# Two attention layers on one core: where the matrix engine passes from one layer to the next

## The chip, the cores and the metric

The kernel runs on one core of one Trainium2 chip. Time is device time in microseconds (us), the median of several executions. Beside it stands one profiled execution, from whose trace all durations below are taken. A core has a matrix engine (PE, with its weight loads shown apart as PEld), a vector engine (DVE), an activation engine (ACT), a general engine (POOL) and a queue that issues most DMAs (SP).

## What is computed

The input x is (4, 128, 64, 64): four batches of 128 channels and 4096 positions. All numbers are 32-bit floats. Layer 0 is an attention of 64 channels with a residual; layer 1 turns to tokens, takes a layer norm, a causal attention of 128 channels with a residual, another norm, and a recurrence over the tokens with batch statistics.

```python
q, k, v = wq @ x, wk @ x, wv @ x                 # 64 x 4096 per batch
att = softmax(einsum('bmi,bmj->bij', k, q), axis=2)
x = x + wo @ einsum('bij,bmj->bmi', att, v)      # layer 0
t = tokens(x)                                    # 4096 x 128 per batch
h = layernorm(t)
t = t + causal_softmax((h Wq)(h Wk)^T / sqrt(128)) @ (h Wv)   # layer 1
w = batchnorm(layernorm(t) @ W^T)
y_t = sigmoid(w_t + y_{t-1} @ V^T)               # over 4096 steps
x = channels(t + y)
```

## The kernel before, in words

Only `fast_path` matters here; `general_path` is a branch that runs when a check of the numbers fails. The end of `fast_path` (the recurrence, from line 1113 on) is untouched by the change.

**Blocks and items.** The work of both attentions is one list. For each batch b, `block` (lines 887 to 902) lists four blocks of layer 0, each of 32 items, and then eight blocks of layer 1, the block g having 2(g+1) items: a block is 512 rows of one output (two such halves at once in layer 0), an item is one tile of 128 keys in layer 0 and two tiles in layer 1. The last two items of each layer 1 block lie on the causal diagonal and are shorter (512+384 and 256+128 columns).

**What an item does.** `scores` (904) multiplies keys by rows on PE into a buffer of the pool `ps_s` (two buffers), and ACT takes the exponential of it into `p` (four buffers); on the diagonal POOL then zeroes a triangle. `sums` (943) adds p into `dsum` on DVE, for the denominators. `values` (963) multiplies values by p on PE into `acc`, of which there is one buffer; at the end of a block ACT copies `acc` out. In layer 0 each item's matmuls go to the four 64x64 quarters of the array, four at a time; in layer 1 they use the whole 128x128 array.

**The loop** (1073 to 1106). In slot s the program issues the scores of item s, the values of item s-2 (`SKEW` is 2), the sums of item s, and then at most one waiting step for each layer, or one of the tasks in the list `side`. So where one layer follows the other, scores of the new layer stand between the last values of the old one. `begin` (1061) issues the scores; after the first block of layer 0 it is called one slot early (lines 1075 to 1078).

**The end of a block.** `finish0` (734) folds the denominators, and later `projected0` (646, 64x64 matmuls) applies the output projection to a pair of row groups and `joining` adds the residual, takes the norm (`moments`, `normed`) and writes its transpose `xhT` by DMA. When that projection runs is set by the table `visits` (1012): the projection of layer 0's pair 0, 1, 2 is issued at the end of layer 0's block 1, 2, 3, and that of pair 3 at the end of layer 1's block 2. `finish1` (777) is a chain of steps a few slots apart: denominators and `projected1` (639, 128x128), norm, transposition, and `third` (842), which multiplies by the FFN's W.

**Rows.** `rows()` (1034) prepares the rows of one block, one block in advance, at each block's end. For layer 0 it costs nothing; for layer 1 it is `rows1` (594), one 512-column product `r_ps` on the whole array, copied out by ACT. So the product for layer 1's block 0 is issued at the end of layer 0's block 2, and that for its block 1 at the end of layer 0's block 3.

**The next batch.** `keys(b, m)` (1020) makes the keys, queries (`cols0`, 128x128) and values (`vals0`, 128x64) of a quarter of a batch. For batch 0 they are done before and in layer 0's first slots, for the others in layer 1's blocks from g=3 on, through `side`.

**What is shared.** Every small product above takes its output from `misc` (489), a pool of two PSUM buffers: `kr_ps`, `v_ps`, `r_ps`, `o_ps`, `den_ps`, `wx_ps` and some others. `projected0` takes both at once and holds them until `joined` (662, DVE) has read them.

**What sets the order.** The program's order is a priority: a planner at build time puts the instructions of each engine in a fixed order by its own estimate of when each can run, and keeps the order only where the program pins it. At run time each engine takes its instructions in that order and waits.

Of the kernel before, what the change touches and what calls it, by code (L numbers as in the profile page):

```python
# [359 lines left out]
def fast_path(  # L360
# [27 lines left out]
    NB = N // BLK  # L388
# [92 lines left out]
    with tc.tile_pool(name="batch", bufs=1) as batch, tc.tile_pool(name="rows", bufs=2) as rowp, tc.tile_pool(  # L481
# [35 lines left out]
        bs = [Batch() for _ in range(B)]  # L517
        for bt in bs:
            bt.next = []
            bt.leave = {}  # L520


        def cols0(b, m):
# [109 lines left out]
        def denominators(layer, b, g, own):  # L633
            rec = recs[:, layer, b, ts(g, TPB)]

            tc.keep_in_program_order(nc.vector.tensor_reduce(rec, own.rearrange("p q j -> p j q"), AX.X, ALU.add))
            nc.vector.reciprocal(rec, rec)

        def projected1(agg):

            op = misc("o_ps")
            for j in range(TPB):
                nc.tensor.matmul(op[:, ts(j, P)], lhsT=agg[:, ts(j, P)], rhs=wv1, start=True, stop=True)  # L643
            return op

        def projected0(agg):

            ops = [misc("o_ps") for _ in range(2)]
            for j in range(TPB):
                for r in range(2):  # L650
                    part = slice(r * M, r * M + M)
                    for c in range(2):
                        nc.tensor.matmul(  # L653
                            ops[r][c * M : c * M + M, ts(j, P)],
                            lhsT=agg[part, ds(j * P + c * M, M)],
                            rhs=wo2[part],
                            start=True,
                            stop=True,
                        )
            return ops  # L660

        def joined(layer, b, g, op):

            rec = recs[:, layer, b, ts(g, TPB)]
            for j in range(TPB):
                t = xs[:, b, ds(g * BLK + j * P, P)]
                nc.vector.scalar_tensor_tensor(  # L667
                    t, in0=op[:, ts(j, P)], scalar=rec[:, j : j + 1], in1=t, op0=ALU.mult, op1=ALU.add
                )
# [64 lines left out]
        def finish0(b, pair):  # L734

            agg, den = bs[b].agg, bs[b].den
            own = {}

            def first(k):
                own[k] = folded(den[:, k], False)  # L740

            def joining(g, op):
                mem = []

                def norm():
                    if g == 0:
                        bs[b].xh = batch.tile([P, NT, P], F32, tag="xh", name="xh")
                    normed(b, g, bs[b].xh[:, ts(g, TPB)], *mem.pop())

                def by_channels():  # L750
                    sq = squares(bs[b].xh[:, ts(g, TPB)])
                    by_r = dram2.tile([S, Q, TPB, Q, S], F32, tag="by_r", name="by_r")
                    for q in range(Q):
                        nc.sync.dma_start(
                            out=by_r[:, :, :, q].rearrange("r c j t -> r (c j) t"),
                            in_=sq[ts(q, S)].rearrange("r c j t -> r (c j) t"),
                        )
                    for c in range(Q):
                        nc.sync.dma_start(
                            out=bs[b].xhT[ts(c, S), ts(g, BLK)], in_=by_r[:, c].rearrange("r j q t -> r (j q t)")  # L760
                        )

                yield 1, lambda: joined(0, b, g, op)
                yield 1 + 4 * (g % 2), lambda: mem.append(moments(b, g))
                yield 1, norm
                yield 2, by_channels

            def leave():
                ops = projected0(agg)
                return [joining(2 * pair + k, op) for k, op in enumerate(ops)]  # L770

            bs[b].leave[pair] = leave
            yield 1, lambda: first(0)
            yield 2, lambda: first(1)
            yield 6, lambda: [denominators(0, b, 2 * pair + k, own[k]) for k in range(2)]

        def finish1(b, g):
            agg, den = bs[b].agg, bs[b].den
            mem = {}
            final = b == B - 1 and g == NB - 1  # L780
# [9 lines left out]
            def first():  # L790
                if final:

                    nc.scalar.activation(spare, agg[:, 0:1], AF.Sigmoid)
                denominators(1, b, g, mem["own"])
                joined(1, b, g, projected1(agg))
                if final:
                    warm(9, agg[:, : BLK // 2])
                if b >= BY_C:
                    nc.sync.dma_start(
                        out=x2t[b - BY_C, ts(g, BLK)].rearrange("(j p) c -> p j c", p=P),  # L800
                        in_=xs[:, b, ts(g, BLK)].rearrange("p (j c) -> p j c", c=P),
                    )
                mem["xh"] = wk.tile([P, TPB, P], F32, tag="xh2", name="xh2")
                mem["of"] = moments(b, g)
                if final:
                    in_range(True)
# [59 lines left out]
            def sums():  # L866
                mem["own"] = folded(den, by_pe)

            if by_pe:
                yield 1, lambda: (sums(), first(), final and norm())  # L870
            else:
                yield 1, sums
                yield 3, first
# [2 lines left out]
            yield 2, second  # L876
            if b < BY_C:
                yield 1, kept
            yield 1 if final else 6 if g < 2 or g == NB - 1 else 4, third


        class Item:
# [2 lines left out]
        items, blocks = [], []  # L885
# [10 lines left out]
        for b in range(B):  # L896
            for g in range(NB // 2):
                block(0, b, g, range(NT))
            for g in range(NB):
                full = [((t, 0, BLK), (t + 1, 0, BLK)) for t in range(0, TPB * g, 2)]  # L900
                d = [(TPB * g + r, r * P, BLK - r * P) for r in range(TPB)]
                block(1, b, g, full + [(d[0], d[1]), (d[2], d[3])])
# [106 lines left out]
        waiting = [[], []]  # L1009


        visits = [{1: 0, 2: 1, 3: 2}, {2: 3}]
        assert NB == 8

        def push(slot, layer, chain):
# [4 lines left out]
        def keys(b, m):  # L1020
# [4 lines left out]
                lambda: b or vals0_by_tokens(b, m, mem[0]),  # L1025
            ]

        parts = [keys(0, m) for m in range(NB // 2)]
        for task in parts[0][:2] + parts[1][:1] + parts[0][2:]:
            task()  # L1030
        SKEW = 2
        side = parts[1][1:] + parts[2] + parts[3] + [form]

        def rows():

# [20 lines left out]
        started = []  # L1056
        rows()
        rows()
        done = -1

        def begin(s):
            nonlocal done
            if done < s < len(items):
                done = s
                it = items[s]
                if it.first:
                    bs[it.b].rows = bs[it.b].next.pop(0)
                    if it.layer and it.g == 3 and it.b + 1 < B:
                        for m in range(NB // 2):
                            side.extend(keys(it.b + 1, m))  # L1070
                scores(it)

        for s in range(len(items) + SKEW + 16):
            begin(s)
            if SKEW < s < len(items) - 1 and items[s - SKEW].first and items[s + 1].layer == 0:
                ended = items[s - SKEW - 1]
                if ended.layer == 0 and ended.g not in visits[0]:
                    begin(s + 1)
            if 0 <= s - SKEW < len(items):
                it = items[s - SKEW]  # L1080
                values(it)
                if it.last:
                    if it.g in visits[it.layer]:
                        for chain in bs[it.b].leave[visits[it.layer][it.g]]():
                            push(s, 0, chain)
                    rows()
                    tokens()
                    push(s, it.layer, (finish1 if it.layer else finish0)(it.b, it.g))
            if s < len(items):
                sums(items[s])  # L1090
            busy = False
            for layer in range(2):
                due = [w for w in waiting[layer] if w[0] <= s]
                if due:
                    busy = True
                    w = min(due, key=lambda w: w[0])
                    waiting[layer].remove(w)
                    w[1]()
                    push(s, layer, w[2])
            if side and not busy:  # L1100
                side.pop(0)()
                if not side and items[s].b == 0 and items[s].layer == 0:
                    tokens()
                    load_rest()
                    form_half()
        assert not any(waiting) and not side


# [213 lines left out]
```

## Time and profile before

| | |
|---|---|
| median of 3 runs | 2058.08 us (2057.14 to 2059.81) |
| the profiled execution | 2057.13 us |
| its span, first to last instruction | 2055.4 us |
| PE busy | 2026.6 us (99%), weight loads 912.4 us |
| DVE busy | 1454.5 us (71%) |
| ACT busy | 976.1 us (47%) |
| POOL busy | 139.8 us (7%) |
| one layer 0 item on PE, from start to start | 1.72 us |
| one full layer 1 item on PE | 3.43 us |

The ends of PE's matmuls in the records are modelled and overlap the next matmul, so "busy" includes waiting time. Starts are observed; the distances between starts are what the text uses.

### The profile page before, as it was taken

What the parts mean: (1) busy time and instruction counts of PE and PEld (TensorE: products, weight loads), DVE (VectorE), ACT (ScalarE), POOL (GpSimd) and SP (SyncE); (2) the same over time, 40 slices, a digit from 0 to 9 for tenths busy, and PEclk for the clock granted to TensorE, in tenths of its full rate; (3) what the DMA queues carried; (4) which work ended last, traced back from release to release, by engine and by line L of the source; (5) the groups of instructions that cost most, each with busy time, mean ns of one, the idle gap of its engine ahead of it and who ended that gap; (6) DMA issues with size and microseconds to landing.
All of it is one profiled execution on the core that took longest, in us unless ns stands there. A gap on an engine that the chain in (4) does not pass through costs nothing.

```text
span 2055.4 us, 31316 instructions
## 1 busy us (share of the span) xinstructions
PE 2026.6 (99%) x11902; PEld 912.4 (44%) x11902; DVE 1454.5 (71%) x2814; ACT 976.1 (47%) x1055; POOL 139.8 (7%) x237
## 2 busy tenths in 40 slices
PE   9999999999999999999999999999999999999998
PEld 3463344444333345444433334444433334444456
DVE  4788887554778877655577888655577887865568
ACT  4665633333666643333466663332356665333346
POOL 1000011000000001000000001000000000100004
PEclk9999999999999999999999999999999999999999
DMA  3101122330011103331110111232000100220046
GB/s 103 53 2 23 22 45 54 69 72 16 17 43 23 19 5 62 72 67 37 20 44 12 22 22 40 54 83 62 16 17 2 18 12 17 55 50 21 16 103 242
DMA packets 238447, 89.06 MB, mean 43 GB/s; under 512 B 174816, under 2 KB 219360, under 8 KB 237776
## 3 DMA queue, kind: packets, MB, share of 16 engines
q1 hardware_dynamic: 237280, 86.42, 17.9%
q8 instruction: 95, 1.56, 0.3%
q14 instruction: 64, 0.52, 0.1%
q0 software_dynamic: 288, 0.39, 0.1%
q10 hardware_dynamic: 720, 0.16, 0.0%
HBM read 45.84 MB, written 36.89 MB: 40 GB/s over the span
## 4 chain that ended last, share of the span: by engine, by line
PE 92%; DVE 4%; ACT 2%; issue 1%; POOL 0%; DVEq 0%; POOLq 0%; ACTq 0%
PE s_ps L926 22%; PE acc L982 22%; PE s_ps L913 20%; PE acc L973 20%; PE o_ps L643 1%; PE r_ps L596 1%; DVE dsum L953 1%; PE kr_ps L534 1%; PE wx_ps L854 1%; DVE z L1188 1%; PE v_ps L546 1%; ACT y L1192 1%; PE o_ps L653 0%; DVE xr L1224 0%; ACT p L920 0%
## 5 line engine op out<-in xcount | busy, mean ns | idle before, releaser
L953 DVE TENSOR_TENSOR dsum<-dsum,p 128x1024 f32<-128x1024 f32 x692 | 845.6, 1222 | 462.2 <-ACT p L929 289.5
L920 ACT ACTIVATE p<-s_ps,nshift 128x1024 f32<-128x1024 f32 x512 | 570.0, 1115 | 314.4 <-PE s_ps L913 288.7
L973 PE MATMUL acc<-p,v 64*64 64x512 f32 x4096 | 643.4, 591 | 0.0
L913 PE MATMUL s_ps<-kr,swap 64*64 64x512 f32 x2048 | 585.8, 591 | 0.3
L913 PE MATMUL s_ps<-kr 64*64 64x512 f32 x2048 | 580.2, 591 | 0.0
L929 ACT ACTIVATE p<-s_ps 128x1024 f32<-128x1024 f32 (+2 forms) x288 | 274.2, 952 | 592.8 <-PE s_ps L926 568.1
L982 PE MATMUL acc<-p,xh 128*128 128x512 f32 (+3 forms) x1152 | 501.1, 558 | 1.4 <-ACT half L996 1.4
L926 PE MATMUL s_ps<-rows,xhT 128*128 128x512 f32 (+3 forms) x1152 | 501.8, 559 | 0.0
L982 PEld LDWEIGHTS acc<-p,xh 128*128 128x128 f32 x1152 | 215.9, 190 | 245.5 <-issue 232.7
L926 PEld LDWEIGHTS s_ps<-rows,xhT 128*128 128x128 f32 x1152 | 214.4, 190 | 247.7 <-issue 208.1
L973 PEld LDWEIGHTS acc<-p,v 64*64 64x64 f32 x4096 | 205.1, 133 | 260.5 <-issue 239.9
L913 PEld LDWEIGHTS s_ps<-kr,swap 64*64 64x64 f32 x2048 | 165.3, 133 | 137.9 <-issue 119.2
L913 PEld LDWEIGHTS s_ps<-kr 64*64 64x64 f32 x2048 | 163.3, 133 | 130.7 <-issue 120.3
L681 POOL TENSOR_TENSOR ln_rstd<-ln_var,mhalf 128x4 f32<-128x4 f32 x64 | 68.2, 1066 | 907.8 <-DVE ln_var L679 907.8
L961 DVE TENSOR_TENSOR dsum<-dsum,p 128x256 f32<-128x256 f32 (+1 forms) x120 | 55.6, 495 | 51.6 <-POOL p L933 51.6
L933 POOL TENSOR_SCALAR_AFFINE_SELECT p<-p 128x128 f32<-128x128 f32 x128 | 36.3, 307 | 602.7 <-ACT p L929 589.3
L667 DVE SCALAR_TENSOR_TENSOR xs<-o_ps,recs,xs 128x128 f32<-128x128 f32 x256 | 70.6, 343 | 3.4 <-PE o_ps L643 0.3
L697 DVE TENSOR_SCALAR xh<-xs,ln_mv,ln_rstd 128x128 f32<-128x128 f32 x252 | 70.0, 341 | 1.8
L676 DVE BATCH_NORM_STATS2 ln_st<-xs 128x6 f32<-128x128 f32 x256 | 64.4, 270 | 0.0
L951 DVE COPY dsum<-p 128x1024 f32<-128x1024 f32 x44 | 30.2, 686 | 28.9 <-ACT p L929 25.6
L859 ACT COPY xs<-wx_ps 128x512 f32<-128x512 f32 x31 | 18.1, 585 | 65.2 <-DVE stats L855 62.0
L596 PE MATMUL r_ps<-xhT,g 128*128 128x512 f32 x64 | 33.6, 607 | 14.2 <-issue 10.4
(149 smaller groups left out, 916.5 us busy)
## 6 DMA issues: line engine op xcount, KB each, us to landing
xs<-in_xT SPq DMA_DIRECT2D x32, 256.0 KB, 3.3
by_r<-sqT SPq DMA_DIRECT2D x128, 64.0 KB, 2.2
xhT<-by_r SPq DMA_DIRECT2D x128, 64.0 KB, 2.0
by_c<-sqT SPq DMA_DIRECT2D x124, 64.0 KB, 1.8
xhT<-by_c SPq DMA_DIRECT2D x31, 256.0 KB, 2.8
xs<-in_x SPq DMA_DIRECT2D x12, 512.0 KB, 6.1
swap<-kr SPq DMA_DIRECT2D x32, 128.0 KB, 2.3
x2c<-sqT SPq DMA_DIRECT2D x64, 64.0 KB, 2.2
```

Source lines behind the costliest of these rows:

```text
L667: nc.vector.scalar_tensor_tensor(t, in0=op[:, ts(j, P)], scalar=rec[:, j : j + 1], in1=t, op0=ALU.mult, op1=ALU.add)
L676: nc.vector.bn_stats(st[:, j], xs[:, b, ds(g * BLK + j * P, P)])
L681: nc.gpsimd.tensor_tensor(y, var, mhalf, ALU.pow)
L697: nc.vector.tensor_scalar(dst[:, j], xs[:, b, ds(g * BLK + j * P, P)], mv[:, j, 0:1], y[:, j : j + 1], ALU.subtract, ALU.mult)
L913: nc.tensor.matmul(ps[c * M : c * M + M, ts(r, BLK)], lhsT=keys[:, ts(c, M)], rhs=rows[r], start=True, stop=True,)
L920: nc.scalar.activation(it.p, ps, AF.Exp, bias=nshift)
L926: nc.tensor.matmul(ps[:, off : off + n], lhsT=lhsT, rhs=rhs, start=True, stop=True)
L929: nc.scalar.activation(it.p[:, :off], ps[:, :off], AF.Exp, scale=float(P) ** -0.5)
L953: nc.vector.tensor_tensor(flat, flat, it.p, ALU.add)
L961: nc.vector.tensor_tensor(den[:, h, q0:], den[:, h, q0:], it.p[:, o : o + n], ALU.add)
L973: nc.tensor.matmul(bt.acc[c * M : c * M + M, r], lhsT=bt.v[part, m * TPB + j, h], rhs=it.p[part, ts(c, BLK)], start=it.first, stop=it.last,)
L982: nc.tensor.matmul(bt.acc[:, 0, q0:], lhsT=bt.xh[:, t], rhs=it.p[:, o : o + n], start=it.first and h == 0, stop=it.last and h == 1,)
```

## The change

- The loop holds back the scores of the first two items of a layer (`turns`) until the values of the old layer's last item, and what else is to be done at that point, have been issued. Sums follow the scores by their own counter.
- The projections of layer 0's pairs 0 to 2 become a step of their own block's chain, 12 slots after the block's end (`yield 3, leave`), in place of the table `visits`. Pair 3 is still projected after layer 1's third block.
- The rows of layer 1's first two blocks are both made at the turn, none at the end of layer 0's block 2.
- Layer 1 takes block 1 before block 0.
- Of the next batch's keys, the last quarter is made at the turn to layer 0; there too goes the projection of layer 1's last block. The last block's product with W (`third`) waits in a list `late` until the next turn to layer 1.
- Scores are begun one slot early at every border between two layer 0 blocks.
- At the start the quarter tasks are run together with pauses, and `form_half` runs 12 slots later.

```diff
@@ finish0
             def leave():
-                ops = projected0(agg)
-                return [joining(2 * pair + k, op) for k, op in enumerate(ops)]
-
-            bs[b].leave[pair] = leave
+                for k, op in enumerate(projected0(agg)):
+                    push(now, 0, joining(2 * pair + k, op))
+
             yield 1, lambda: first(0)
             yield 2, lambda: first(1)
             yield 6, lambda: [denominators(0, b, 2 * pair + k, own[k]) for k in range(2)]
-
-        def finish1(b, g):
+            if pair < NB // 2 - 1:
+                yield 3, leave
+            else:
+                bs[b].leave = leave
+
+        def finish1(b, g, turn):
...
-                joined(1, b, g, projected1(agg))
+                joined(1, b, g, mem["op"] if turn else projected1(agg))
...
+            if turn:
+                mem["op"] = projected1(agg)
             if by_pe:
...
-            yield 1 if final else 6 if g < 2 or g == NB - 1 else 4, third
+            if turn:
+                late.append(third)
+            else:
+                yield 1 if final else 6 if g < 2 else 4, third
...
-            for g in range(NB):
+            for g in (1, 0, *range(2, NB)):
...
-        visits = [{1: 0, 2: 1, 3: 2}, {2: 3}]
...
+        late = []
+        SKEW = 2
         parts = [keys(0, m) for m in range(NB // 2)]
-        for task in parts[0][:2] + parts[1][:1] + parts[0][2:]:
+        for task in parts[0][:2] + parts[1][:1] + parts[0][2:] + parts[1][1:2]:
             task()
-        SKEW = 2
-        side = parts[1][1:] + parts[2] + parts[3] + [form]
+
+        def together(*tasks):
+            return lambda: [task() for task in tasks]
+
+        idle = lambda: None
+        side = [idle, together(parts[1][2], *parts[2][:2]), idle, idle, together(parts[2][2], *parts[3][:2]), idle, idle]
+        side.append(together(parts[3][2], form))
...
-                        for m in range(NB // 2):
+                        for m in range(NB // 2 - 1):
                             side.extend(keys(it.b + 1, m))
                 scores(it)
 
+        def turns(s):
+            return SKEW <= s < len(items) and items[s].layer != items[s - SKEW].layer
+
         for s in range(len(items) + SKEW + 16):
-            begin(s)
-            if SKEW < s < len(items) - 1 and items[s - SKEW].first and items[s + 1].layer == 0:
-                ended = items[s - SKEW - 1]
-                if ended.layer == 0 and ended.g not in visits[0]:
-                    begin(s + 1)
+            now = s
+            if not turns(s):
+                begin(s)
+                if SKEW < s < len(items) - 1 and items[s - SKEW].first and not turns(s + 1):
+                    if items[s].layer == 0 and items[s - SKEW - 1].layer == 0:
+                        begin(s + 1)
             if 0 <= s - SKEW < len(items):
                 it = items[s - SKEW]
                 values(it)
                 if it.last:
-                    if it.g in visits[it.layer]:
-                        for chain in bs[it.b].leave[visits[it.layer][it.g]]():
-                            push(s, 0, chain)
-                    rows()
+                    turn = turns(s)
+                    if it.layer == 0:
+                        push(s, 0, finish0(it.b, it.g))
+                        if turn:
+                            rows()
+                        if not blocks[0][0] or turn:
+                            rows()
+                        while turn and late:
+                            late.pop(0)()
+                    else:
+                        if it.g == 2:
+                            waiting[0].append((s + 1, bs[it.b].leave, iter(())))
+                        if turn:
+                            held = keys(it.b + 1, NB // 2 - 1)
+                            held[0]()
+                        push(s, 1, finish1(it.b, it.g, turn))
+                        if turn:
+                            held[1]()
+                        rows()
                     tokens()
-                    push(s, it.layer, (finish1 if it.layer else finish0)(it.b, it.g))
-            if s < len(items):
-                sums(items[s])
+                    if turn:
+                        begin(s - 1)
+                        begin(s)
+            while summed < min(done, s):
+                summed += 1
+                sums(items[summed])
...
-                    form_half()
+                    waiting[0].append((s + 12, form_half, iter(())))
```

More of the change, by code (lines that the diff above doesn't have):

```diff
@@ L519, in fast_path @@
             bt.next = []
-            bt.leave = {}
         def cols0(b, m):
@@ L1058, in fast_path @@
         rows()
-        done = -1
+        done = summed = -1
         def begin(s):
```

## Prediction

> **What bounds the kernel now.** I read the page's engine shares and chain first, then PE's own waits, then the timeline at every place where PE falls behind its steady pace.
>
> ```profile
> PE 2026.6 (99%) x11902; PEld 912.4 (44%) x11902; DVE 1454.5 (71%) x2814; ACT 976.1 (47%) x1055; POOL 139.8 (7%) x237
> PE 92%; DVE 4%; ACT 2%; issue 1%; POOL 0%; DVEq 0%; POOLq 0%; ACTq 0%
> ```
>
> PE is both the busy engine and the chain. But matmul ends are modelled, so I measure start to start and set it against the work. A 512-column matmul takes 0.427 us (four of them are a steady 1.71 us group in layer 1), four 64x64 quarters sharing one such time; 128-column ones a quarter of it. From 8 to 1975 us the distances between PE's starts add up to about 47 us more than that, the steady pace's own few ns per matmul taken off. The change can win only from those 47 us. Where they lie:
>
> ```profile
> PE r_ps L596 <- issue: 10.4, 4, 2.6
> PE r_ps L596 <- PE acc L982: 3.9, 4, 1.0
> ```
>
> PE's two largest waits: the rows product of layer 1, twice per batch, 14.3 us in all. The timeline at the end of layer 0's third block, batch 1:
>
> ```profile
> 686.68 1.05 PE L653 MATMUL o_ps<-wo,xhT 64*64 64x128 f32 x32
> 687.55 0.60 PE L913 MATMUL s_ps<-kr,swap 64*64 64x512 f32 x2
> ...
> 689.96 2.15 DVE L667 SCALAR_TENSOR_TENSOR xs<-o_ps,recs,xs 128x128 f32<-128x128 f32 x8
> ...
> 691.18 1.10 PE L596 MATMUL r_ps<-xhT,g 128*128 128x512 f32 x2 [2.60 <-issue]
> 692.20 0.64 PE L913 MATMUL s_ps<-kr 64*64 64x512 f32 x1
> ```
>
> The projection (L653) takes both `misc` buffers; r_ps needs one, and the first is free only when four of DVE's eight L667 steps are through (689.96 + 4 x 0.27 = 691.04). PE stands in its fixed order behind r_ps, with a quarter of a score still to do. The turn to layer 1, same batch:
>
> ```profile
> 743.85 1.77 PE L926 MATMUL s_ps<-rows,xhT 128*128 128x512 f32 x4
> 745.55 1.09 PE L973 MATMUL acc<-p,v 64*64 64x512 f32 x8
> 746.57 0.92 PE L926 MATMUL s_ps<-rows,xhT 128*128 128x256 f32 x4
> 747.41 1.09 PE L973 MATMUL acc<-p,v 64*64 64x512 f32 x8
> 748.32 1.05 PE L653 MATMUL o_ps<-wo,xhT 64*64 64x128 f32 x32
> 749.73 2.17 PE L982 MATMUL acc<-p,xh 128*128 128x512 f32 x6 [0.35 <-ACT half L996]
> 751.65 2.15 DVE L667 SCALAR_TENSOR_TENSOR xs<-o_ps,recs,xs 128x128 f32<-128x128 f32 x8
> 752.87 1.10 PE L596 MATMUL r_ps<-xhT,g 128*128 128x512 f32 x2 [0.97 <-PE acc L982]
> 754.89 3.60 PE L926 MATMUL s_ps<-rows,xhT 128*128 128x512 f32 x8
> ```
>
> Five changes of array shape, a wait for `acc`, and the same wait for a `misc` buffer again. The turn to layer 0:
>
> ```profile
> 513.29 0.14 PEld L913 LDWEIGHTS s_ps<-kr,swap 64*64 64x64 f32 x2 [0.76 <-issue]
> 513.29 0.65 PE L913 MATMUL s_ps<-kr,swap 64*64 64x512 f32 x2
> 514.31 1.77 PE L982 MATMUL acc<-p,xh 128*128 128x512 f32 x4
> 516.01 0.65 PE L913 MATMUL s_ps<-kr,swap 64*64 64x512 f32 x2
> ```
>
> Eight quarter matmuls are 0.85 us of work and take 1.02; four full ones of 512+384 columns are 1.49 and take 1.70.
>
> **What the Trainium skill says.** "TensorEngine Tiling (Array Packing)", Key Properties: changing the tiling mode, not just the tile, drains the engine. The trace agrees and prices it: 0.11 to 0.21 us per change, 0.16 on average. "TensorE: Matmul & The Clock Gate", Architectural detail: PE can pull weight loads ahead of running matmuls. In steady stretches the trace shows them 0.43 us ahead; at the change above load and matmul both start at 513.29, so the price is lost prefetch as well as drain. "Trainium Kernel Development and Optimization", Best Practices: steady bubbles can mean that PSUM ran out; the r_ps wait is that. "Perfetto Trace Analysis" says that PE ends are estimated, hence starts here.
>
> **Part by part.**
>
> *Third block and turn to layer 1* (rows moved, pairs' projections moved, scores held back). From the projection at the third block's end to the first full layer 1 scores after r_ps, PE takes 68.21 us in batches 1 to 3 (686.68 to 754.89) and 69.90 in batch 0, for 61.44 of work; steady loss over some 68 groups is 0.4. Avoidable: 6.4, 6.4, 6.4, 8.1, sum 27.2 us. Of a 6.4, 3.2 is the third block (687.55 to 692.20 is 4.65 us for 1.49 of work), the rest the turn. Batch 0's extra 1.7 follows its r_ps, when quarters run out of step.
> What stays: at the turn PE does the last two values, two r_ps, `late` (0.86 us; none in batch 0), then scores. The last values need no wait: their exponential ends about 1.4 us after the scores (0.2 + 1.11), PE has 1.7 us of other values. One change of shape, 0.3 with the lost prefetch. ACT copies `acc` (1.00), then the first rows (0.59): ready about 2.0 us after the last values, PE gets there after 1.7 to 2.6: 0 to 0.3. New: with only two items of block 0 after block 1, r_ps of block 2 is needed at once; its copy waits behind `agg` (0.58) and itself takes 0.8, PE has 0.86 of r_ps and perhaps 1.5 of values: 0 to 0.8. I take 0.9 in all. PE executes in order, so each of these holds up all that follows it on PE, and through the scores ACT's exponentials. The projections themselves stay 0.87 us each, now amid 64x64 work without a change. Gain 27.2 - 4 x 0.9 = 23.6.
>
> *Turn to layer 0, three times.* Losses from 511.5 to 545: alternating 1.07, the projection at 525.14 0.51, W's product at 543.55 0.37; 1.95, of which 0.2 stays (the 128-column loads). After: 128x128, then v_ps in 128x64, then 64x64, two changes (0.35); the projection waits for a `misc` buffer that DVE empties (0.69 + 0.2, against 0.86 of PE work; 0.1); and the pipe refills: two scores are 1.72 us, the first exponential is ready at 0.86 + 0.2 + 1.11 + 0.1 = 2.3, so 0.5. Sum 1.0. In layer 1 one of four v_ps insertions goes (0.3). Gain 3 x (1.75 - 1.0 + 0.15) = 2.7; the 0.15 halves that 0.3, as the quarter's swap and value DMAs (10 more on SP at the turn) might delay token loads. The quarter is needed 24 items later, 41 us, so that they land late matters only past that.
>
> *Start.* Some 8 fewer changes x 0.16 = 1.3, and `form_half` no longer right behind its loads (36 to 41 us loses 0.9). Against it, three bundled tasks chain through two `misc` buffers, 0.2 to 0.9 each. Between -1.5 and +2; I take a gain of 0.7.
>
> *Block borders in layer 0.* Early scores replace the projection as the work that covers the copy of `acc` (1.00 us against 1.72). Block 0's border does so today: 575.56 to 578.99 is exactly four steady groups. 0. If ACT were late there, about 0.5 each, 8 borders.
>
> *DVE.* A pair's chain (joining, moments, norm, transpose; about 13 us with the folds, from the L667, L676, L677, L697, L711, L607, L609 rows) no longer starts with the folds of the next block. Spare DVE time in layer 0 is 1.72 - 1.22 = 0.5 us per slot, and four p buffers hide about 5 us of lag; today it shows as 0.4 us once in three of the batches. Taken as 0, between -2 and +1.2.
>
> Sum: 23.6 + 2.7 + 0.7 = 27.0 us. Against the profiled execution: span 2055.4 to 2028.4, 2057.1 to 2030.1. The median is 0.95 above the profiled run, so 2031.
>
> **Rivals.**
> 1. *Gain half eaten by refills.* At each of seven turns nothing fills PE while the exponential (and POOL's triangles) and ACT's rows copy come. Worst case at a turn to layer 1: 1.4 before the last values, 1.9 for the copies, 0.8 for block 2's rows, 4.1 against 0.9 taken; to layer 0: 1.3 + 1.8 for two evacuations + 1.3, 4.4 against 1.0. Half of that excess is 4 x 1.6 + 3 x 1.7 = 11.5: 2042. For: the planner misjudged r_ps today. Against: the drain's own arithmetic above.
> 2. *The changes of shape alone go, the r_ps waits return elsewhere.* 27.0 - 14.3: 2045.
> 3. *Slower.* The two `misc` buffers collide in layer 1's start: pair 3's projection, W's products of blocks 0 and 1, and the next rows fall within four slots after block 2, while DVE is near full (24.5 busy of 26 us from 764 to 790 today). Each wait costs 3 us like the r_ps one; more than nine, some two or three per batch, cancel the gain; at four per batch, 16 x 3 = 48, 2079. Against: today the same steps meet there (790 to 800) at under 0.2 us each, and 10 us of DVE work, pair 2's chain, leaves that stretch.
> 4. *Nothing*: within 0.2% if the waits only change their names, 2058.
>
> **Numbers.** Likeliest 0.68 (2031, its own range 2024 to 2039), rivals 1 and 2 0.19 together, no change 0.04, slower 0.09. About 0.2% (4 us) is what a measurement of this kernel can tell. Faster 0.87, same 0.04, slower 0.09. The range 2024 to 2047 takes the likeliest and rivals 1 and 2.
>
> **What would show it.** r_ps waits of PE from 14.3 to under 3 us; no 128x128 matmul inside layer 0's 32-item blocks after batch 0's start; 68.21 us becoming about 62.7; one wait of about half a microsecond early in each turn to layer 0. Wrong if new PE waits on `misc` users (o_ps, wx_ps, den_ps) appear in layer 1's first 40 us, or if DVE's lag holds up exponentials after the moved projections.

## The result and the profile after

The changed kernel takes 2028.26 us (median of 4 runs, 2028.15 to 2028.38); the kernel before, on the same chip, takes 2058.03 (4 runs, 2057.14 to 2059.81). The ratio is 0.9854, with a 95% interval of 0.9837 to 0.9871. The forecast was 2031.0, within 2024 to 2047. The profiled execution took 2028.15 us with a span of 2026.4, against 2055.4 before: 29.0 us less.

The page of the kernel after, its engine shares and its chain:

```profile
PE 2011.7 (99%) x11902; PEld 878.3 (43%) x11902; DVE 1459.6 (72%) x2814; ACT 975.9 (48%) x1055; POOL 139.8 (7%) x237
PE 96%; DVE 2%; ACT 2%; DMA 0%; issue 0%; POOL 0%; ACTq 0%; POOLq 0%
```

The same 11902 matmul records; the chain still runs along PE, and DVE's and ACT's shares of it fell from 6% to 4%. One fp32 matmul stands as two records in the trace: layer 0's 512 items make four score matmuls each, and L920 has 4096 records. The prediction's "eight quarter matmuls" are eight such records, four matmuls. PE's waits after (what waits, for what, us in total, times, longest):

```profile
PE warm_ps L495 <- POOL ident masks.py:199: 2.6, 1, 2.6
PE s_ps L920 <- ACT p L927: 1.3, 3, 0.4
```

The two `r_ps` rows, 14.3 us before, are gone. No wait of the attention's blocks is left but the second row: three of 0.4, one per turn to layer 0. The first lies at the program's start, and the rows below these, 1.1 us and less each, at its start and in its last part.

The timeline at the end of layer 0's third block, batch 1 (start, duration, engine, line, operation), where PE stood for 2.60 us before:

```profile
679.61 0.60 PE L920 MATMUL s_ps<-kr,swap 64*64 64x512 f32 x2
...
680.04 1.90 PE L980 MATMUL acc<-p,v 64*64 64x512 f32 x16
681.75 0.60 PE L920 MATMUL s_ps<-kr 64*64 64x512 f32 x2
```

Scores go straight into sixteen value records and back: 1.71 us from 680.04 to 681.75 for 1.71 of work. The turn to layer 1, batch 0:

```profile
245.98 2.75 PE L980 MATMUL acc<-p,v 64*64 64x512 f32 x24
...
248.67 1.98 PE L595 MATMUL r_ps<-xhT,g 128*128 128x512 f32 x4
248.81 1.01 ACT L1003 COPY half<-acc 128x1024 f32<-128x1024 f32 x1 [1.46 <-PE acc L980]
...
249.83 0.59 ACT L597 COPY rows<-r_ps 128x512 f32<-128x512 f32 x1
...
250.49 5.18 PE L933 MATMUL s_ps<-rows,xhT 128*128 128x512 f32 x12
```

One change of shape where there were five. ACT's copies end at 250.42 and the scores start at 250.49, 1.82 us after `r_ps`, whose four records are 1.71 of work: 0.11 lost. The turn to layer 0, batch 1:

```profile
509.34 0.65 PE L920 MATMUL s_ps<-kr,swap 64*64 64x512 f32 x2
...
511.72 0.65 PE L920 MATMUL s_ps<-kr,swap 64*64 64x512 f32 x2 [0.44 <-ACT p L927]
```

The half-microsecond wait that the prediction placed here is in the last line. The list counts 0.44 from a modelled end; from start to start it is 0.60. The records are drawn 0.6 long where the pace is 0.43, so other waits behind PE's own work are short by about as much in these lists.

As in the prediction, I call loss the time between PE's starts less the work in it; here it is taken over the whole program, and the steady pace's few ns per matmul are left in, so that the sum before is 70 where the prediction spoke of 47. By stage (items are those of the named layer), in us:

| stage | before | after | difference |
|---|---|---|---|
| start to layer 0's item 20, batch 0 | 7.73 | 8.88 | +1.15 |
| batch 0, items 20 to 44 | 0.53 | 0.26 | -0.27 |
| layer 0's items 44 to 90, four batches | 2.93 | 1.92 | -1.01 |
| third block and turn to layer 1, to item 20, four | 35.13 | 9.02 | -26.11 |
| layer 1's items 20 to 60, batches 0 to 2 | 7.58 | 6.32 | -1.26 |
| layer 1's item 60 to layer 0's item 20, three | 6.71 | 5.13 | -1.58 |
| everything else | 9.48 | 9.52 | +0.04 |
| sum | 70.09 | 41.05 | -29.04 |

Nine tenths of the gain lies in one stage. The start is the one place that got worse.

Of the 35.13 before, 1.7 is neither a wait nor a change of shape. In batch 0, 1.4 us after the end of the 2.6 us wait for `r_ps`, the trace has a stretch with half the granted clock (window, length, busy time of PE, PEld, DVE, ACT and POOL, granted clock, DMA):

```profile
198.89:202.30 3.41, 3.41 (x20) 1.07 (x16) 2.44 (x13) 1.39 (x2) 1.01 (x1) 0.50 0.02 2
```

Groups of four records start 0.85 us apart there (199.01, 199.87, 200.72) in place of 0.43; 3.41 us at half speed cost 1.7. This is the "extra 1.7" of batch 0 that the prediction put down to quarters running out of step. The kernel after has no such stretch between its start and its last microseconds.

### The profile page after: what moved, and what is told of

Its sections match the earlier page's. It is cut to its first block, busy times and chain, and to the rows that moved or that the text cites. A ratio compares the mean times of both kernels' runs of the same rounds, so it can differ in the third digit from the quotient of the medians.

```text
span 2026.4 us, 31276 instructions
## 1 busy us (share of the span) xinstructions
PE 2011.7 (99%) x11902; PEld 878.3 (43%) x11902; DVE 1459.6 (72%) x2814; ACT 975.9 (48%) x1055; POOL 139.8 (7%) x237
## 4 chain that ended last, share of the span: by engine, by line
PE 96%; DVE 2%; ACT 2%; DMA 0%; issue 0%; POOL 0%; ACTq 0%; POOLq 0%
PE s_ps L933 22%; PE acc L989 22%; PE s_ps L920 22%; PE acc L980 22%; PE o_ps L642 1%; PE r_ps L595 1%; PE wx_ps L856 1%; PE kr_ps L533 1%; DVE z L1223 1%; PE v_ps L545 1%; PE o_ps L652 1%; ACT y L1227 1%; DVE xr L1259 0%; ACT xs L1227 0%; PE warm_ps L495 0%; DMA swap<-kr 0%
## 5 line engine op out<-in xcount | busy, mean ns | idle before, releaser
L980 PE MATMUL acc<-p,v 64*64 64x512 f32 x4096 | 530.2, 589 | 0.0
L920 PE MATMUL s_ps<-kr,swap 64*64 64x512 f32 x2048 | 524.7, 590 | 1.9 <-ACT p L927 1.3
L920 PE MATMUL s_ps<-kr 64*64 64x512 f32 x2048 | 522.5, 590 | 0.0
L980 PEld LDWEIGHTS acc<-p,v 64*64 64x64 f32 x4096 | 157.3, 133 | 282.8 <-issue 274.5
L920 PEld LDWEIGHTS s_ps<-kr,swap 64*64 64x64 f32 x2048 | 142.0, 133 | 146.2 <-issue 135.7
L920 PEld LDWEIGHTS s_ps<-kr 64*64 64x64 f32 x2048 | 141.7, 133 | 135.4 <-issue 133.9
L710 DVE STREAM_TRANSPOSE sqT<-xh 128x512 f32<-128x512 f32 x63 | 44.7, 709 | 1.7
L1223 DVE SCALAR_TENSOR_TENSOR z<-xs,scale,y_ps 128x256 f32<-128x256 f32 x100 | 43.5, 477 | 1.8 <-PE y_ps L1221 1.6
```

Of the source, the lines that this page charges most:

```text
L920: nc.tensor.matmul(ps[c * M : c * M + M, ts(r, BLK)], lhsT=keys[:, ts(c, M)], rhs=rows[r], start=True, stop=True,)
L980: nc.tensor.matmul(bt.acc[c * M : c * M + M, r], lhsT=bt.v[part, m * TPB + j, h], rhs=it.p[part, ts(c, BLK)], start=it.first, stop=it.last,)
L1223: ins = nc.vector.scalar_tensor_tensor(grid(z), in0=wx, scalar=scale, in1=grid(ps), op0=ALU.mult, op1=ALU.add)
```

## The experiments

My theory: of the gain, half is the wait for a `misc` buffer behind `r_ps`, and the rest is mainly changes of shape. The runs bear out the first half alone. The rivals that were still to be told apart: that holding back the scores does the work, that the block order does, or that moving the projections does it alone. The first four kernels start from the kernel before or price one term; the next five take one part out of the kernel after, and the last goes further at one turn.

**The wait alone.** Kernel before, with layer 1's rows issued ahead of the pair's projection, so that they take their buffer first:

```diff
                 if it.last:
+                    if it.layer == 0:
+                        rows()
                     if it.g in visits[it.layer]:
...
-                    rows()
+                    if it.layer:
+                        rows()
```

> The kernel before, with one edit: at the end of a layer 0 block the rows product is issued ahead of the pair's projection, so r_ps takes a misc buffer first. Array shapes change as often as before. If the 3.2 us at the third block and the 1.0 us at the turn are the wait for a misc buffer (my account): the r_ps waits of 14.3 us go, but the projection now waits for one buffer until ACT has copied the rows, up to about 1 us each time; 8 to 14 us faster, 2044 to 2050. If r_ps waited for its data (xhT by DMA) or the loss is the change of shape: within 2 us of before.

Measured: 2043.29 us (2042.82 to 2043.85), ratio 0.9927 [0.991, 0.9943]: 15.0 us gained, a shade more than forecast; by the traces 1.7 of it is the half-clock stretch, which is gone with the wait. No `r_ps` wait remains. Its timeline at the third block's end, batch 1:

```profile
682.11 1.13 PE L596 MATMUL r_ps<-xhT,g 128*128 128x512 f32 x2
683.16 1.54 PE L653 MATMUL o_ps<-wo,xhT 64*64 64x128 f32 x26
...
684.54 0.49 PE L653 MATMUL o_ps<-wo,xhT 64*64 64x128 f32 x6
```

`r_ps` runs without a wait; now the projection waits for its second buffer, but only for ACT's one copy of the rows, and its 32 records (0.85 of work) go in two runs. So the wait is a matter of who holds the two buffers and for how long: behind ACT's 0.60 us copy it is short, behind four of DVE's eight steps it was 2.6. That is half the gain, by moving one call. It is a net sum: at each turn to layer 1 the projection still takes 1.77 us for its 0.85 (742.11 to 743.88 in batch 1), and PE's stream has 119 changes of shape where before had 111.

**Projections amid the blocks alone.** Kernel before, with pairs 0 to 2 projected in their own chain 12 slots on, and scores begun early at each border that this frees:

```diff
@@ finish0
-                return [joining(2 * pair + k, op) for k, op in enumerate(ops)]
+                    push(now, 0, joining(2 * pair + k, op))
...
+            if pair < NB // 2 - 1:
+                yield 3, leave
...
@@ the loop
-                if ended.layer == 0 and ended.g not in visits[0]:
+                if ended.layer == 0:
                     begin(s + 1)
```

> The kernel before, with the projections of pairs 0 to 2 moved 12 slots into the next block and early scores at all layer 0 borders; rows, turns, start and the order of blocks stay. Buffer theory: both r_ps waits go (14.3 us) with batch 0's 1.6 us out of step and the 0.4 us lost at each drain after it; 16 to 19 us faster, 2039 to 2042, and what the whole change gains beyond that (11 to 14 us) is held-back scores, fewer changes of shape and the wait for acc. Shape theory (the changes are the main loss): under 8 us, for r_ps still stands amid 64x64 work.

Measured: 2034.03 us (2033.66 to 2034.53), ratio 0.9881 [0.9865, 0.9898]: 24.3 of the 29.8 us, where 16 to 19 were expected. Counted over the trace, PE's stream has 111 changes of shape here, as many as before, so none of the 24.3 comes from fewer changes. That is against the second half of my theory: what the whole change gains beyond this run is 5.5, where I had expected 11 to 14. The turn to layer 1, batch 1, in this kernel:

```profile
734.36 1.77 PE L929 MATMUL s_ps<-rows,xhT 128*128 128x512 f32 x4
736.06 1.09 PE L976 MATMUL acc<-p,v 64*64 64x512 f32 x8
...
737.93 1.09 PE L976 MATMUL acc<-p,v 64*64 64x512 f32 x8
738.95 1.98 PE L596 MATMUL r_ps<-xhT,g 128*128 128x512 f32 x4
```

The interleaving of both layers is still there and costs 0.9 (5.56 us from 733.39 to 738.95 for 4.69 of work). Gone, beside the `r_ps` waits, are the wait for `acc` and the projection that stood in the turn, so the third block with the turn loses 3.2 instead of 8.3 (in batch 0, with the half-clock stretch, 3.4 instead of 9.9). What is left beyond these waits, about 1 us a batch, is not split further. Layer 0's items 44 to 90, where the folds and the pair's chain met on DVE, fell from as much as 0.86 to 0.48 a batch in the same run.

**Holding back the scores alone.** Kernel before, with the loop's `turns` and nothing else:

```diff
+            if not turns(s):
+                begin(s)
...
+                    if turns(s):
+                        begin(s - 1)
+                        begin(s)
```

> The kernel before, with the scores of a new layer held back at the seven turns, nothing else. Four changes of shape fewer at each turn are worth 7 x 4 x 0.16 = 4.5 us, the wait for acc another 1.4. But at the turn to layer 1 the projection holds both misc buffers ahead of r_ps with nothing left to run behind it, so PE should wait there about 3 us instead of 1.0. My account: between 4 us faster and 6 us slower, 2054 to 2064, with r_ps waits over 18 us. If held-back scores are the main source of the gain: 10 us or more faster.

Measured: 2055.6 us (2053.79 to 2056.6, 20 runs), ratio 0.9985 [0.9978, 0.9992]. PE's waits in it:

```profile
PE r_ps L596 <- issue: 10.4, 4, 2.6
...
PE r_ps L596 <- PE s_ps L926: 1.9, 4, 0.5
```

Only 2.7 us: without the moved projections the buffer wait stays, 12.3 us of it. It did not grow as I had expected, because the planner let a score of block 0 run ahead of the second `r_ps`.

The 2.7 is a net sum too, and says too little of the held-back scores. By the trace the turns to layer 1 lose 6.4 less and those to layer 0 0.7 less, but the third blocks lose 4.5 more: from the end of the `r_ps` wait on the granted clock was 0.50 for 3.41 us in batches 1 and 2 and for 6.83 in batch 3, against one such stretch of 3.41 in the profiled run before. The 10.2 us more at half speed cost some 5.1, an estimate. Among the twelve traces such stretches, outside the start and the end of a program, occur in these two kernels alone, the two that keep the 2.6 us wait. That the wait brings them on is likely but was not tested by itself.

**The price of a change of shape.** Kernel after, with 32 extra products of 16 columns on the whole array in layer 0's blocks, which nothing reads: 64 more changes.

```diff
+                if it.layer == 0 and it.tile in (24, 28):
+                    dp = misc("dummy_ps")
+                    nc.tensor.matmul(dp[:, :16], lhsT=ident, rhs=ident[:, :16], start=True, stop=True)
```

> The changed kernel with 32 extra products of 16 columns on the whole array, two in each layer 0 block at items 24 and 28, whose output nobody reads: 64 extra changes of shape and 0.03 us of work each. At 0.11 to 0.21 us per change the pair costs 0.27 to 0.40 with the work: 9 to 13 us slower, 2037 to 2041. If a change costs only the drain of the array (below 0.08 us each): under 6 us slower. If lost order behind it costs more (exponentials late): over 16.

Measured: 2044.17 us (2043.42 to 2044.5), 15.9 above the kernel after, 0.50 for each insertion; more than expected. Its timeline at one of them:

```profile
557.69 1.04 PE L980 MATMUL acc<-p,v 64*64 64x512 f32 x8
558.66 0.40 PE L1125 MATMUL dummy_ps<-ident 128*128 128x16 f32 x2
...
558.98 0.65 PE L920 MATMUL s_ps<-kr,swap 64*64 64x512 f32 x2
...
559.89 1.04 PE L980 MATMUL acc<-p,v 64*64 64x512 f32 x8
```

Eight quarters take 0.97 (work 0.85), the product 0.32 (0.03), the next eight 0.91 (0.85): 0.46 beyond the work for a change and back. "TensorEngine Tiling (Array Packing)", Key Properties, in the Trainium skill says that a new mode drains the engine; this run agrees that a change costs time. But 0.23 for each change is too much, for a short product costs something without any change. The kernel after has one between products of the same shape:

```profile
752.85 0.29 PE L614 MATMUL den_ps<-part,fold 128*128 128x16 f32 x2
752.99 1.14 PE L642 MATMUL o_ps<-wv,agg 128*128 128x128 f32 x8
```

It takes 0.14 for 0.03 of work. With these 0.11 taken off, 0.35 is left for the two changes, an estimate of at most 0.17 to 0.18 each, as the long groups at the turns of before (0.17 to 0.21).

**The order of the two blocks.** Kernel after, with layer 1's block 0 first again:

```diff
-            for g in (1, 0, *range(2, NB)):
+            for g in range(NB):
```

> The changed kernel with layer 1's blocks in the order 0, 1, 2. Two short diagonal items come first after the turn: 0.64 us of scores, then the next scores wait for the first exponential (about 0.5 us), and the first block's agg copy is waited for sooner. My account: 0.5 to 1.2 us lost per batch, 2 to 5 us slower, 2030 to 2033. If the order of the two blocks does nothing: within 0.7 us of 2028.3. If it keeps r_ps of block 2 from being late, as I priced: up to 2 us faster.

Measured: 2029.71 us (2028.96 to 2030.49). By the trace the third block and turn lose 2.08 to 2.40 instead of 2.23 to 2.33, hardly any difference; most of what the run is longer lies at the start (9.34 against 8.88). The order of the two blocks is worth next to nothing.

**The start.** Kernel after, with the quarter tasks one at a time as before; `form_half` stays 12 slots later:

```diff
-        for task in parts[0][:2] + parts[1][:1] + parts[0][2:] + parts[1][1:2]:
+        for task in parts[0][:2] + parts[1][:1] + parts[0][2:]:
...
-        side = [idle, together(parts[1][2], *parts[2][:2]), idle, idle, together(parts[2][2], *parts[3][:2]), idle, idle]
-        side.append(together(parts[3][2], form))
+        side = parts[1][1:] + parts[2] + parts[3] + [form]
```

> The changed kernel with the start of before (the quarter tasks one per slot, the second quarter's values not ahead of the loop), form_half still 12 slots later. The trace after loses 7.1 us between the first keys and 90 us, before lost 5.5, so that the bundled start looks 1.6 us worse, where I had forecast 0.7 better. If the bundles are the cause: 1.2 to 2.5 us faster, 2026 to 2027. If the loss is chance of the loads: within 0.5 us.

Measured: 2026.57 us (2025.88 to 2027.11), ratio to before 0.9846 [0.9829, 0.9862]. This is the best version of all: its median is 1.7 below that of the kernel after, though the kernel before took 2058.71 beside it. To item 20 it loses 6.76 against 8.88. The kernel after at that place:

```profile
18.49 1.07 PE L920 MATMUL s_ps<-kr,swap 64*64 64x512 f32 x2
19.49 1.12 PE L533 MATMUL kr_ps<-xs,wqk 128*128 128x512 f32 x2
20.54 1.07 PE L920 MATMUL s_ps<-kr,swap 64*64 64x512 f32 x2
21.54 1.08 PE L545 MATMUL v_ps<-xs,wv 128*64 128x512 f32 x4
```

The bundle did not stay a bundle. Between its products, which follow each other through two `misc` buffers, the planner put one of a score's four matmuls. Its two records run one after the other on one quarter of the array (20.54 and 21.02), and the other three quarters stand empty: 1.00 us from start to start for what is 0.21 of work when four matmuls run side by side, three times. The first, at 13.16, also waited 0.63 for the DMA of `swap`, a wait that the trace of the old start hasn't; so some of the 2.12 may be the chance of the loads.

**The borders of layer 0.** Kernel after, with early scores only after block 0, as before:

```diff
-                    if items[s].layer == 0 and items[s - SKEW - 1].layer == 0:
+                    if items[s].layer == 0 and items[s - SKEW - 1].layer == 0 and items[s - SKEW - 1].g == 0:
                         begin(s + 1)
```

> The changed kernel with early scores at the border after layer 0's block 0 alone. At the 8 other borders inside layer 0 no projection covers the copy of acc any more, PE has one score product (0.86 us) for a copy of 1.0 us behind an exponential. My account: 0.5 us each, 3 to 6 us slower, 2031 to 2034. If the planner finds other work: within 0.7 us.

Measured: 2033.35 us (2032.76 to 2034.6), 5.1 above the kernel after, 0.64 at each of 8 borders. Its waits have a row that the kernel after hasn't:

```profile
PE acc L980 <- ACT half L1003: 3.4, 8, 0.4
```

At the first of two such borders in batch 1 the values start at 624.72, when ACT's copy of `acc` is done, 0.6 late; the rest is lost just after. So the early scores are the cover that the prediction named when it put this step at nothing.

**The turn to layer 0, filled as before.** Kernel after, but with the last quarter of keys in the list `side` and the last block's projection and product with W back in its chain; the scores are still held back:

```diff
-                yield 1 if final else 6 if g < 2 else 4, third
+                yield 1 if final else 6 if g < 2 or g == NB - 1 else 4, third
...
-                        for m in range(NB // 2 - 1):
+                        for m in range(NB // 2):
...
-                        push(s, 1, finish1(it.b, it.g, turn))
...
+                        push(s, 1, finish1(it.b, it.g, False))
```

> The changed kernel with the turn to layer 0 filled as before: the last quarter of keys in layer 1, the last block's projection and product with W in layer 0's first block; scores still held back. Back come 2 changes of shape each for the projection (0.4 us) and the product with W (0.37), and 0.3 for v_ps in layer 1; the turn itself saves about 0.4. My account: 0.5 to 0.9 us per turn, 1.5 to 2.7 us slower, 2030 to 2031. If the placement does nothing: within 0.5 us.

Measured: 2030.1 us (2029.92 to 2030.71), 1.8 above the kernel after, as expected. By the trace 0.36 of it per batch is the one insertion of `v_ps` that returns to layer 1's blocks (2.47 against 2.11), 0.30 the turn.

**The turn to layer 0 without holding back.** Kernel after, with the scores of layer 0 in their usual place:

```diff
-            if not turns(s):
+            if not turns(s) or items[s].layer == 0:
                 begin(s)
```

> The changed kernel with the scores of layer 0's first two items no longer held back at the turn to layer 0 (three turns); keys, projections and rows stay where the change put them. Four or five changes of shape more per turn at 0.2 us, 0.8 to 1.0, against the refill wait that the trace after shows there, 0.6: 0.2 to 0.4 us per turn, 0.5 to 1.5 us slower, 2028.8 to 2029.8. If held-back scores were the heart of the gain: over 4 us slower.

Measured: 2031.25 us (2030.73 to 2031.71), 3.0 above the kernel after, 1.0 a turn, more than expected. By the trace 0.58 of it is lost at the turn itself, where PE's stream has 8 changes of shape in place of 2; the rest follows in layer 0's blocks and at the next turn. Beside the changes, one matmul of a score stands alone between the keys and `projected1` at 509.28 and takes 1.00: the same fragment as at the start.

**More values at the turn.** The kernel of the old start, with the values of quarters 1 to 3 all made at the turn to layer 0:

```diff
-                            side.extend(keys(it.b + 1, m))
+                            side.extend(nxt[m] if m == 0 else nxt[m][:1])
...
-                            held[1]()
+                            for m in (1, 2, 3):
+                                nxt[m][1]()
```

> The changed kernel with the start of before, and of the next batch's values the quarters 1, 2 and 3 all made at the turn to layer 0 in place of the last alone. Two insertions of the 128x64 shape fewer in each of three layer 1 runs, 0.29 us each in the trace after: 1.7 us. Against the same start without this (2026.6): 2025 if nothing else moves; slower than it, 2028 or more, if the three quarters' 24 DMAs at the turn hold up the denominators or DVE's transposes hold up PE.

Measured: 2031.55 us (2030.55 to 2031.81), 5.0 above the kernel with the old start. Two fewer insertions gain 0.7 per batch in layer 1 (2.11 to 1.40), but the turn loses 3.98 instead of 1.71:

```profile
503.79 1.08 PE L545 MATMUL v_ps<-xs,wv 128*64 128x512 f32 x4
504.80 1.07 PE L920 MATMUL s_ps<-kr,swap 64*64 64x512 f32 x2
505.80 1.08 PE L545 MATMUL v_ps<-xs,wv 128*64 128x512 f32 x4
```

Between two `v_ps` one matmul of a score goes in, at 1.00 us for 0.21 again, twice per turn. My reading is that the planner expects the next `v_ps` to have no buffer yet, so that filling a turn pays only as far as two buffers carry it; a run with a third buffer, which would show it, was not made.

## Why the prediction was right, point by point

**Third block and turn to layer 1** (forecast 23.6). The stretch that the prediction defined lost 25.8 us less over four batches. The mechanism was right, and the runs split it: the `r_ps` wait alone is worth 15.0, moving the projections 24.3. One reading of it was wrong: batch 0's extra 1.7 is the half-clock stretch, not quarters out of step. It was counted among the avoidable and did go, which says nothing for the reason given. The term that was mis-sized is what stays at the turn: 0.9 was taken, and some 0.36 was measured (0.76 lost a batch, less the steady 0.4); the 68.21 us became 62.2 where 62.7 was named. The copy of the rows is ready when PE gets to it, and the feared 0 to 0.8 for block 2's rows never shows in the waits.

**Turn to layer 0 and the insertions of `v_ps`** (forecast 2.7). Measured 1.58 + 1.26 = 2.84. The parts are shared out differently: the whole 0.4 of an insertion was kept where half of 0.3 was taken, and the turn gave less, 0.5 each instead of 0.75. The refill was forecast at half a microsecond and is 0.60 from start to start.

**Start** (forecast a gain of 0.7; between -1.5 and +2). This step failed in sign. It rested on some 8 fewer changes of shape at 0.16; the trace has 6 fewer. `form_half` did give what was put down: before, a score split by its products lost 1.16 at 37.47, and this is gone. But scores were cut into fragments, 0.79 lost in each of three, and the kernel without the bundles is faster. I had priced the chain through two buffers as waiting, and not asked what the planner would put into the gaps. PE's first product also started 0.76 us earlier in the profiled run after than in the one before (7.07 against 7.83; 7.44 in the kernel with the old start), but its first score no earlier (13.16 against 13.14), behind the wait for `swap`.

**Borders in layer 0** (0) held, and taking the cover away cost 0.64 each where 0.5 had been named. **DVE** (0, between -2 and +1.2): its lag vanished, 1.0 us. **A change of shape** (0.16) held, as far as the runs show. PE's stream has 55 of them after, counted over the whole trace, and had 111 before. The run with the projections moved alone still has 111; from it to the kernel after, the third block and turn lose 3.2 and then 2.3 a batch with 9 and then 3 changes: 0.16 for each that goes, if all of it is put down to them. So the gain is not half waiting and half changes, as my theory had it: 24.3 come without a change fewer, and the 56 changes, at 0.16 some 9 us by estimate, are in the main what makes up the other 5.5, less what the fragments at the start and the refills take back.

**The sum.** 27.0 us were forecast and 29.8 measured, and part of that nearness is luck: the start came out 1.9 worse than forecast, while the third block and turn gave 2.2 to 2.5 more and DVE 1.0. The step from the profiled run to the median, 0.95 before, was carried over to the kernel after, where it is 0.11.

**The rivals.** Refills ate little (rival 1): 0.60 at each turn to layer 0. That the waits come back elsewhere (rival 2) did not happen: no wait for a `misc` buffer is among PE's waits after. Neither do `o_ps`, `wx_ps` or `den_ps` appear there in layer 1's start, which rival 3 needed. Rival 4 (nothing) is excluded by the interval.

**What would show it.** All four signs came: `r_ps` is out of PE's waits, the stretch is 62.2 us, each turn to layer 0 has its half-microsecond wait, and no whole-array product stands inside layer 0's blocks after batch 0's start, where the trace of before had ten.

## What to carry to other kernels

Where PE stops for "issue" at the end of a block, look for who holds the few PSUM buffers of the small products: a product whose result a slow engine reads in many steps belongs in the middle of a block, and whatever a fast engine frees should be issued ahead of it. Work collected at a turn between two shapes paid here as long as it ran through; with more of it, the planner put pieces of the other shape in between, and the turn cost more than it saved. Before putting a gain down to fewer changes of shape, count them in each run: the run that gained most from one part had as many as before. Measure PE from start to start against its work and price each stage before and after, since the busy share read 99% in both kernels; and where a stretch runs at half the pace, look at the granted clock of that window before explaining it by the order of the work.

## What the runs showed of the hardware that was not expected

- One fp32 64x64 matmul of 512 columns that stands alone between other shapes takes 1.00 us from start to start (20.54 to 21.54), where four of them together take 0.85 in a steady stretch and 1.02 between other shapes (before, turn to layer 0).
- A product of 16 columns costs 0.46 to 0.50 us when it interrupts a stretch of another shape, and 0.14 between products of its own shape (752.85).
- The weight load runs about 0.43 us ahead of its matmul in the steady stretches of before and after; at a change of shape both start together (513.29 in the prediction's lines).
- In the profiled run before, the granted clock was 0.50 for 3.41 us just after one of four 2.6 us waits of PE; in the run with held-back scores alone, for 13.7 us in all at three of them.
